# Entry into a state-space block: an order of steps for its first pair, another PSUM ring for its side line, other buffers for its time-step weights

## The chip, the cores and the metric

The kernel runs on one core of one Trainium2 chip. The metric is the device time of one execution in microseconds (us); less is better. Three executions of the kernel before took 2607.37, 2610.11 and 2611.04 us; their median is 2610.11 us. One more execution was taken with the profiler running; all views of the profile are of that one.

TensorE is called PE in the profile, VectorE DVE, ScalarE ACT, GpSimd POOL, and the engine that issues the DMAs SP. "PEld" is the weight load of PE. Each engine works through its own instructions strictly in the order in which they stand; what it needs from another engine it waits for.

## The reference, cut to what matters

The reference runs two layers over 4 sequences of 256 tokens with 512 features. Every step has a residual connection and takes the layer norm of its input:

```python
x = x + _L0_attn_ref(_layernorm(x), ...)   # block 1: gated retention, 32 heads
x = x + _L0_ffn_ref(_layernorm(x), ...)    # block 2: router, 64 experts' biases
x = x + _L1_attn_ref(_layernorm(x), ...)   # block 3: state space, 128 heads of 64
x = x + _L1_ffn_ref(_layernorm(x), ...)    # block 4: adapters of rank 16
```

Block 3, where the change lies, is in essence:

```python
proj = x @ in_proj_w.T                    # gate 8192 | x 8192, B 1024, C 1024 | dt 128
hBC = silu(causal_conv4(proj[x, B, C]) + conv_b)
hs, B, C = split(hBC)                     # 128 heads of 64; 8 groups of 128
dt = clip(softplus(proj[dt] + dt_bias), 0, 100);  A = -exp(A_log)
# in chunks of 128 tokens, two per sequence:
Y = (C B^T * exp(segsum(dt * A))) (hs * dt) + carried state + hs * D
g = Y * silu(gate);  g = g * rsqrt(mean of g^2 over each group + eps) * norm_w
out = g @ out_proj_w.T
```

The time step `dt` of every head and token is needed before anything can be decayed, so the 128 rows of `in_proj_w` that make it (the time-step weights) are used ahead of all else in this block.

## The kernel before

**Halves.** The 8 token tiles are worked in two halves of 4 tiles (512 tokens). `k.xs[half]` holds the normalized, turned input as a high and a low part; every projection (`proj`, L200) is 12 matmuls with 512 columns: four pieces of the contraction times three products (high by high, low by high, high by low).

**Weights.** All large weights go through `Weights`: a DMA into a `raw` buffer on SP, then `split` (L138 on ACT for the high part, L141 on POOL for the low part) into rings of three buffers (tag "w") or two ("wo"). A cast into a ring buffer waits until PE has used the weight that was there.

**Block 3 in pairs.** One *pair* is one group, one pair of channel chunks and one half. The first eight pairs are four pairs of half 0 and then the same four of half 1 (`FIRST3 = 1`). For each `i` the loop in `run` overlaps three pairs: `before`, `p` and `after`. Its order is written out by hand as letters. `B` projects B and C of a group, convolves them (L707 ACT, L709 DVE) and makes the products `cb` (L728 PE, L732 ACT). `I0 I1` project and convolve x, `G0 G1` project the gates (tile `ps_g`, silu on ACT), `X0 X1` load the cumulated decays and add them up (`exponents`, L286, L293, L295), `D0 D1` exponentiate them and multiply by `cb` (L1110 ACT, L748 DVE). `T0 T1` turn x (L770, L772, L781), `M0 M1` are the mixing matmuls `ps_y` (L795) with L805, L809, L813 and L814 behind them, `O0` to `O3` are the output projection `ps_o` (L849, L855). `W` takes the next weight, `P` and `E` pump the side line.

**The side line.** Work that belongs to other blocks is a list of generators, `k.side`, and is worked off in small steps in between. As soon as a half has left block 1, `route(half)` (block 2) and then `prepare3(half)` (L676: time-step weights, layer norm, `steps_of` for dt and its cumulated sum) are put on it. While block 3 works on its first pairs, half 1 is still in the side line: its router (`ps_xn` L107, `ps_lg` L596, a softmax and top 8 on DVE, `ps_t` L627, `ps_o` L642), its norm (`ps_xn` again) and its time steps (`ps_dt` L200, `ps_v` L220, `ps_cum` L249, `ps_in` L258, `ps_tail` L267). All of them must be through before the first pair of half 1. Every step of the side line takes its PSUM tile from the ring that `k.bank` names. There are four rings of two banks each: "x" (projections of x, B, C, and `cb`), "g" (gates), "y" (turned x and `ps_y`), "o" (output). In block 1 the side line uses "o"; in block 3, and in the preparation of block 4 that runs beside its last pairs (`prepare4`), it uses "x". `first(c)` of block 4 always takes ring "g".

**Which list holds.** At `i = -1` there is no pair to mix yet and only `after` has work:

```python
STEP3 = "W T0 T1 B I0 W M0 M1 X0 X1 I1 O0 G0 W W O1 W W P O2 W W G1 P W O3 D0 D1 W W".split()
SIDE3 = "T0 T1 I0 I1 M0 M1 P B X0 X1 P P O0 W O1 G0 G1 W W P O2 O3 W P W P D0 D1 E E".split()
for one in SIDE3 if k.side else STEP3:
```

**Scheduler.** The letters give the order of the program. A scheduler then places the instructions on the engines' queues by its own model of their durations, within what the tiles' buffers allow: a tile in a ring of two can't be written before the tile two places earlier in that ring has been read.

Of the kernel before, what the change touches and what calls it, by code (L numbers as in the profile page):

```python
# [11 lines left out]
F32 = mybir.dt.float32  # L12
F32R = mybir.dt.float32r
AF = mybir.ActivationFunctionType
ALU = mybir.AluOpType
# [3 lines left out]
P = 128  # L19
NB, SEQ, HID = 4, 256, 512  # L20
NT = NB * SEQ // P
KC = HID // P
HT = NT // 2
FREE = HT * P
EPS = 1e-5
GONE = -30000.0
YB = 3
LONE1, FIRST3, LONE3 = 3, 1, 2
PUMP = 1
AHEAD = 0  # L30
BANK1, BANK3 = "o", "x"
LATE = (0, 3)
STEP1 = "K S0 W T S1 S2 W G0 G1 K C K P U A0 K W P A1 T P P Q0 N0 W W N1 Q1 T T W K D F".split()
SIDE1 = "S0 W G0 T P K C W W P P W S1 K G1 S2 U P A0 N0 A1 P Q0 T W T F W N1 K Q1 T T D W W".split()
STEP3 = "W T0 T1 B I0 W M0 M1 X0 X1 I1 O0 G0 W W O1 W W P O2 W W G1 P W O3 D0 D1 W W".split()
SIDE3 = "T0 T1 I0 I1 M0 M1 P B X0 X1 P P O0 W O1 G0 G1 W W P O2 O3 W P W P D0 D1 E E".split()


# [72 lines left out]
def normalize(k, tc, half, tag, into=("xn",)):  # L111


    nc = tc.nc
    tiles = [HT * half + at for at in range(HT)]
    of = [moments(k, tc, t, tag) for t in tiles]
    ahead = len(into)
    xns = [centre(k, tc, tiles[at], of[at], tag, into[at]) for at in range(ahead)]
    yield
    for at, t in enumerate(tiles):  # L120
        xn = xns[at]
        ps = turned(k, tc, xn, f"xn_{tag}_{t}")
        hi, lo = (part[:, :, at * P:at * P + P] for part in k.xs[half])
        nc.scalar.copy(hi, ps)
        nc.vector.tensor_tensor(lo, ps, hi.bitcast(F32), ALU.subtract)
        if at + ahead < HT:
            xns.append(centre(k, tc, tiles[at + ahead], of[at + ahead], tag, into[at % ahead]))
        yield


def split(k, tc, w, name, tag, late=False):

    nc = tc.nc
    n = w.shape[1]
    bufs = 3 if tag == "w" else 2
    hi = k.wp.tile([P, 2, HID], F32R, tag=tag + "h", name=f"{name}_h", bufs=bufs)[:, 0:n, :]
    lo = k.wp.tile([P, 2, HID], F32R, tag=tag + "l", name=f"{name}_l", bufs=bufs)[:, 0:n, :]
    high = nc.scalar.copy(hi, w)  # L138
    if late:
        tc.keep_in_program_order(high)  # L140
    nc.gpsimd.tensor_tensor(lo, w, hi.bitcast(F32), ALU.subtract)  # L141
    return hi, lo
# [506 lines left out]
def state_space(k, tc, io):  # L649


    nc = tc.nc
    NH, NG, D = 128, 8, 64
# [22 lines left out]
    def prepare(half):  # L676

        if half == 0:
            yield True
            k.act(amp, amp, AF.Exp)  # L680
            nc.vector.tensor_scalar_mul(amp, amp, -1.0)
        raw = k.wk.tile([P, 1, FREE], F32, tag="xn", name=f"raw_wdt_{half}", bufs=1)
        nc.sync.dma_start(raw, io["L1_attn_in_dt"])
        yield
        wd = split(k, tc, raw, f"wdt_{half}", "w")
        yield from normalize(k, tc, half, "3")

        def room(size, name):
            if half == 0:
                return k.const.tile([P, size], F32, name=f"{name}3_0")  # L690
            return own.only.tile([P, size], F32, name=f"{name}3_1")

        dt[half] = room(HT * NH, "dt").rearrange("p (t h) -> p t h", t=HT)
        start[half] = room(3 * 2 * NH, "start").rearrange("p (k h b) -> p k h b", k=3, b=2)
        yield from steps_of(
            k, tc, half, [part[:, 0, :].rearrange("p (c m) -> p c m", c=KC) for part in wd], NH,
            bias, amp, 100.0, dt[half].rearrange("p (b z) h -> p b z h", b=2), start[half],
            cum[half], "3", "y" if half else "a",
        )
        ready.add(half)  # L700
# [14 lines left out]
    def group(p):  # L715

        g, half = p.g, p.half
        bc = [
            k.wk.tile([P, FREE], F32, tag="y", name=f"bc_{g}_{half}_{n}", bufs=4) for n in range(2)
        ]  # L720
        for n, first in enumerate((BS, CS)):
            conv(proj(k, tc, chunk(p.w.bc(), n), half, f"bc_{g}_{half}_{n}"), bc[n], first + g)
        s = own.only.tile([P, 3, 2, P], F32, tag="cb", name=f"cb_{g}_{half}", bufs=2)
        for b in range(2):
            ps = k.psum.tile([P, 3, P], F32, tag="x", name=f"ps_cb_{g}_{half}_{b}")
            for n, (zs, zl) in enumerate(((0, 0), (1, 1), (0, 1))):
                fs, fl = (2 * b + zs) * P, (2 * b + zl) * P
                nc.tensor.matmul(  # L728
                    ps[:, n, :], bc[0][:, fs:fs + P], bc[1][:, fl:fl + P],
                    start=True, stop=True,  # L730
                )
            nc.scalar.copy(s[:, :, b, :], ps)  # L732
        cbs[g, half] = s

    def sums(p, n):
        hs = slice(2 * (p.ch + n), 2 * (p.ch + n) + 2)
        p.e[n] = exponents(
            k, tc, cum[p.half][:, hs, :], start[p.half][:, :, hs], f"{p.name}_{n}", 2
        )
# [15 lines left out]
    def inputs(p, n):  # L755
        xs = k.wk.tile([P, FREE], F32, tag="a", name=f"xs_{p.name}_{n}", bufs=4)
        conv(proj(k, tc, chunk(p.w.x(), n), p.half, f"x_{p.name}_{n}"), xs, p.ch + n)
        p.xs.append(xs)

    def gate(p, n):  # L760
        sg = k.wk.tile([P, FREE], F32, tag="sg", name=f"sg_{p.name}_{n}", bufs=4)
        k.act(sg, proj(k, tc, chunk(p.w.g(), n), p.half, f"g_{p.name}_{n}", "g"), AF.Silu)
        p.sg.append(sg)
# [73 lines left out]
    def output(p, t):  # L837
        if p.cp == 0 and t == 0:
            acc[p.g, p.half] = k.wk.tile([P, HT, HID], F32, tag="big", name=f"acc_{p.name}")
        if p.cp == NC // 2 - 1 and t == 0:  # L840
            scale(p)
        ps = k.psum.tile([P, HID], F32, tag="o", name=f"ps_o3_{p.name}_{t}")
        at = slice(t * P, t * P + P)
        i = 0
        for n in range(2):
            yh, yl = p.y[n]
            wh, wl = p.w.o()
            for y, w in ((yh, wh), (yh, wl), (yl, wh)):
                nc.tensor.matmul(ps, y[:, at], w[:, n, :], start=(i == 0), stop=(i == 5))  # L849
                i += 1  # L850
        a = acc[p.g, p.half][:, t, :]
        if p.cp == 0:
            nc.scalar.copy(a, ps)
        else:
            nc.vector.tensor_tensor(a, a, ps, ALU.add)  # L855
        if p.cp == NC // 2 - 1:
            xt = k.x[HT * p.half + t]
            nc.vector.scalar_tensor_tensor(xt, a, p.r[:, t:t + 1], xt, ALU.mult, ALU.add)  # L858
# [8 lines left out]
    for together in order:  # L867
        pair = [(*divmod(n, NC // 2), half) for half in range(2) for n in together]
        for g, cp, half in pair:
            p = Ctx()  # L870
# [13 lines left out]
    def run(done):  # L884


        with tc.tile_pool(name="s3", bufs=1, reuse_waits="tile") as own.only:
            for i in range(-1, len(pairs) + 1):
                k.bank = BANK3
                before, p, after = (  # L890
                    pairs[j] if 0 <= j < len(pairs) else None for j in (i - 1, i, i + 1)
                )
                if i + 2 < len(pairs):
                    k.weights.due = pairs[i + 2].w.g.n
                else:
                    k.weights.due = len(k.weights.all) - 1
                if after is not None and after.half not in ready:
                    k.pump(1000, True)

                def shared():  # L900
                    if after.cp == 0:
                        group(after)

                def put(t):
                    output(before, t)
                    if t == HT - 1 and all(one.half != before.half for one in pairs[i:]):
                        done(before.half)

                step = dict(
                    B=shared, I=lambda n: inputs(after, n), G=lambda n: gate(after, n),  # L910
                    X=lambda n: sums(after, n), D=lambda n: decays(after, n), T=lambda n: turn(p, n), M=lambda n: mixer(p, n),
                    O=put, W=k.weights.step, P=k.pump, E=lambda: k.pump(1, True),
                )
                for one in SIDE3 if k.side else STEP3:
                    who = {"T": p, "M": p, "O": before, "P": k, "E": k, "W": k}.get(one[0], after)
                    if who is not None and (i >= 0 or not AHEAD or one[0] not in "IG"):
                        step[one[0]](*(int(n) for n in one[1:]))

    def ahead(i):
# [8 lines left out]
        else:  # L928
            sums(p, n)

    return ahead, prepare, run


# [309 lines left out]
```

## Time and profile before

| | |
|---|---|
| median of three executions | 2610.11 us (2607.37 to 2611.04) |
| the profiled execution | 2612.82 us, of which the span from first to last instruction is 2611.1 us |
| busy: PE, DVE, ACT, POOL | 2475.6, 2082.7, 1533.4, 1530.1 us |
| mean granted TensorE clock | 0.978 |
| first matmul of block 3 | 923.2 us after the start |
| first projection of block 3 from which both kernels' PE queues are alike again (second x of group 1, pair 0, half 1) | 1238.8 us |
| last matmul | 2607.2 us |

A row of "busy time in stretches" gives a stretch, its length, the busy time of PE, PE's weight loads, DVE, ACT and POOL with their instruction counts, the granted TensorE clock, the busy share of the DMA engines and their rate. Rows of a timeline give the start, the duration, the engine, the line, the operation with its output and inputs, the number of instructions, and in square brackets how long the engine stood idle before it and who released it. Durations of matmuls are pipelined: 12 projection matmuls that stand one behind another take 2.80 us together, although each row says 0.40 us.

### The profile page before, as it was taken

The numbers are of one execution on the slowest core, as the hardware profiler recorded it, in microseconds if no ns is written. First come the engines' busy times: TensorE is split into PE (matmuls) and PEld (weight loads), VectorE is DVE, ScalarE is ACT, GpSimd is POOL, SyncE is SP. The second block draws the span as 40 slices with busy tenths as digits, with TensorE's granted clock in tenths as the row PEclk, the third lists the DMA queues.
The fourth block names the chain that finished last, engine by engine and source line by source line (L and its number), as shares of the span: only waits on it lengthen the run. The fifth ranks groups of instructions, "written<-read, shape, count | busy, mean of one in ns | idle before, by whom it ended". The sixth has DMA issues, their size and how long they took to land.

```text
span 2611.1 us, 35577 instructions
## 1 busy us (share of the span) xinstructions
PE 2475.6 (95%) x13488; PEld 2001.8 (77%) x13488; DVE 2082.7 (80%) x2694; ACT 1533.4 (59%) x2109; POOL 1530.1 (59%) x996
## 2 busy tenths in 40 slices
PE   7899999999999888889999999999999999999889
PEld 5677787788777676668878788788787887887667
DVE  5678777778789767688897988888888878879963
ACT  2556556566665555465765665756757657657631
POOL 4445444546565445577674874765756766757840
PEclk9899999999999988999999999999999999999989
DMA  3212111212221222232322222323222222313221
GB/s 105 74 49 65 57 49 56 58 59 87 88 93 57 77 89 69 69 108 86 98 90 65 89 89 68 103 65 89 95 75 89 89 69 88 101 61 104 90 77 67
DMA packets 82891, 206.18 MB, mean 79 GB/s; under 512 B 8672, under 2 KB 10592, under 8 KB 82720
## 3 DMA queue, kind: packets, MB, share of 16 engines
q1 hardware_dynamic: 82720, 203.90, 25.3%
q8 instruction: 107, 1.75, 0.3%
q14 instruction: 64, 0.52, 0.1%
HBM read 200.86 MB, written 3.01 MB: 78 GB/s over the span
## 4 chain that ended last, share of the span: by engine, by line
PE 60%; DVE 24%; ACT 6%; POOL 5%; issue 4%; DMA 2%; SPq 0%; POOLq 0%; ACTq 0%; DVEq 0%
PE ps_g L200 12%; PE ps_o L849 8%; PE ps_x L200 6%; PE ps_o L458 6%; PE ps_q L200 6%; DVE conv L709 5%; DVE m L748 5%; PE ps_y L795 3%; PE ps_y L411 3%; PE ps_sc L399 2%; DVE x L858 2%; PE ps_bc L200 2%; DVE m L293 2%; PE ps_v L200 2%; PE ps_h L200 2%
## 5 line engine op out<-in xcount | busy, mean ns | idle before, releaser
L200 PE MATMUL ps_g<-xs_hi,wg_h 128*128 128x512 f32 x768 | 309.8, 403 | 17.5 <-ACT wg_h L138 7.3
L200 PE MATMUL ps_g<-xs_lo,wg_h 128*128 128x512 f32 x768 | 305.5, 398 | 0.0
L200 PE MATMUL ps_g<-xs_hi,wg_l 128*128 128x512 f32 x768 | 304.1, 397 | 1.2 <-POOL wg_l L141 1.2
L748 DVE TENSOR_TENSOR m<-m,cb 128x1536 f32<-128x1536 f32 x128 | 263.8, 2073 | 47.8 <-ACT m L1110 43.4
L709 DVE SCALAR_TENSOR_TENSOR conv<-ps_x,cw,conv 128x510 f32<-128x510 f32 (+2 forms) x384 | 271.1, 739 | 17.6 <-ACT conv L707 14.4
L1107 ACT ACT_TABLE_LOAD x193 | 247.6, 1283 | 4.0 <-PEq L1231 0.8
L141 POOL TENSOR_TENSOR wo_l<-raw_wo,wo_h 128x1024 fp32r<-128x1024 f32 x60 | 154.6, 2578 | 136.6 <-ACT wo_h L138 136.5
L293 POOL TENSOR_TENSOR m<-gb,start 128x512 f32<-128x512 f32 x128 | 152.9, 1197 | 137.6 <-PE ps_y L795 94.4
L1110 ACT ACTIVATE xs<-conv,cb 128x512 f32<-128x512 f32 x128 | 91.8, 724 | 239.6 <-DVE conv L709 236.6
L809 POOL TENSOR_TENSOR xs<-xs,sg 128x512 f32<-128x512 f32 x128 | 201.2, 1572 | 42.9 <-DVE xs L805 42.3
L849 PE MATMUL ps_o<-wo_h,yh 128*128 128x512 f32 x512 | 213.0, 416 | 9.8 <-DVE acc L855 6.9
L295 POOL TENSOR_SCALAR_AFFINE_SELECT m<-m 128x1024 f32<-128x1024 f32 x160 | 216.7, 1355 | 0.8 <-DVE m L293 0.7
L200 PE MATMUL ps_x<-xs_hi,wx_h 128*128 128x512 f32 x512 | 206.4, 403 | 7.8 <-DVE conv L709 7.8
L849 PE MATMUL ps_o<-wo_h,yl 128*128 128x512 f32 x512 | 201.1, 403 | 6.3 <-DVE yl L814 6.2
L200 PE MATMUL ps_x<-xs_lo,wx_h 128*128 128x512 f32 x512 | 204.9, 400 | 0.0
L200 PE MATMUL ps_x<-xs_hi,wx_l 128*128 128x512 f32 x512 | 203.6, 398 | 0.0
L849 PE MATMUL ps_o<-wo_l,yh 128*128 128x512 f32 x512 | 203.2, 397 | 0.0
L823 POOL TENSOR_TENSOR sqs<-sqs,sq 128x512 f32<-128x512 f32 x112 | 174.7, 1560 | 48.5 <-ACT sq L821 48.1
L141 POOL TENSOR_TENSOR wx_l<-raw_wx,wx_h 128x1024 fp32r<-128x1024 f32 x38 | 97.8, 2575 | 174.4 <-DVE conv L709 118.7
L795 PE MATMUL ps_y<-m,xd 128*64 128x128 f32 x2048 | 178.2, 280 | 14.5 <-DVE m L748 13.8
L141 POOL TENSOR_TENSOR wg_l<-raw_wg,wg_h 128x1024 fp32r<-128x1024 f32 x60 | 159.1, 2652 | 54.8 <-ACT wg_h L138 52.8
L200 PEld LDWEIGHTS ps_g<-xs_hi,wg_h 128*128 128x128 f32 x768 | 144.8, 189 | 60.2 <-issue 14.9
(281 smaller groups left out, 6975.0 us busy)
## 6 DMA issues: line engine op xcount, KB each, us to landing
gb<-cum SPq DMA_DIRECT2D x160, 512.0 KB
raw_wx<-in_L_attn_in_x_dram SPq DMA_DIRECT2D x38, 512.0 KB
raw_wg<-in_L_attn_in_gate_dram SPq DMA_DIRECT2D x38, 512.0 KB
raw_wo<-n_L_attn_out_proj_w_dram SPq DMA_DIRECT2D x38, 512.0 KB
raw_wq<-in_L_attn_Wq_dram SPq DMA_DIRECT2D x22, 512.0 KB
raw_wg<-in_L_attn_Wg_dram SPq DMA_DIRECT2D x22, 512.0 KB
raw_wo<-in_L_attn_Wo_dram SPq DMA_DIRECT2D x22, 512.0 KB
raw_wkv<-in_L_kv_dram SPq DMA_DIRECT2D x11, 512.0 KB
```

Source lines behind the costliest of these rows:

```text
L141: nc.gpsimd.tensor_tensor(lo, w, hi.bitcast(F32), ALU.subtract)
L200: tc.nc.tensor.matmul(ps, a[:, c, :], b[:, c, :], start=(c == 0 and n == 0), stop=(c == KC - 1 and n == 2))
L293: engine.tensor_tensor(m[:, blk], gb[:, min(blk, 1)], last(at, P), ALU.add)
L295: nc.gpsimd.affine_select(out=causal, in_=causal, compare_op=ALU.is_ge, fill=GONE, base=0, pattern=[[0, 8], [1, P]], channel_multiplier=-1,)
L458: nc.tensor.matmul(ps, y[:, 2 * h + b, :], w[:, h, :], start=(i == 0), stop=(i == 5))
L709: nc.vector.scalar_tensor_tensor(acc[:, :, j:], ps[:, :, :SEQ - j], cw[:, ch, TAPS - 1 - j:TAPS - j], acc[:, :, j:], ALU.mult, ALU.add,)
L748: made = nc.vector.tensor_tensor(mh, mh, cbs[p.g, p.half].rearrange("p z b l -> p z (b l)").unsqueeze(2) .to_broadcast([P, 3, 2, 2 * P]), ...
L795: one = nc.tensor.matmul(ps_y[h * D:h * D + D, 2 * b + z, :], p.xe[:, n, b, h, :] if blk == 2 else xd[:, 2 * b + zs, h, :], m[:, blk, 2 * ...
L809: nc.gpsimd.tensor_tensor(xs, xs, p.sg[n], ALU.mult)
L823: nc.gpsimd.tensor_tensor(total, total, sq, ALU.add)
L849: nc.tensor.matmul(ps, y[:, at], w[:, n, :], start=(i == 0), stop=(i == 5))
L1107: load = nc.scalar.preload_act_table_set(table)
```

## The change

1. At `i = -1` the loop follows a list of its own, `FILL3`: the decays' loads first, B and C ahead of x, and the side line's steps at other places.
2. `BANK3` is "g" instead of "x": the side line of block 3, and the preparation of block 4 that runs beside it, take their PSUM tiles from the gates' ring.
3. The time-step weights of `prepare3` no longer go through `split` and the ring "w". For half 0 the raw block and its two parts take free buffers of the tags "yh" and "yl"; for half 1 the raw block goes into the first 512 columns of `k.room` (the tables of sine and cosine of block 1) and the parts into the ring "y" of four. Tag "xn" no longer holds the raw block.

```diff
-BANK1, BANK3 = "o", "x"
+BANK1, BANK3 = "o", "g"
...
+FILL3 = "X0 X1 B I0 W I1 P P G0 G1 W P P D0 D1 E E".split()
...
-        raw = k.wk.tile([P, 1, FREE], F32, tag="xn", name=f"raw_wdt_{half}", bufs=1)
-        nc.sync.dma_start(raw, io["L1_attn_in_dt"])
+        if half == 0:
+            raw = k.wk.tile([P, FREE], F32, tag="yh", name="raw_wdt_0", bufs=YB)
+        else:
+
+            raw = k.room[:, 0:FREE]
+        nc.sync.dma_start(raw, io["L1_attn_in_dt"][:, 0])
         yield
-        wd = split(k, tc, raw, f"wdt_{half}", "w")
+        tags, bufs = (("yh", "yl"), YB) if half == 0 else (("y", "y"), 4)
+        wd = [
+            k.wk.tile([P, FREE], F32R, tag=tag, name=f"wdt_{half}_{part}", bufs=bufs)
+            for tag, part in zip(tags, "hl")
+        ]
+        nc.scalar.copy(wd[0], raw)
+        nc.gpsimd.tensor_tensor(wd[1], raw, wd[0].bitcast(F32), ALU.subtract)
         yield from normalize(k, tc, half, "3")
...
-            k, tc, half, [part[:, 0, :].rearrange("p (c m) -> p c m", c=KC) for part in wd], NH,
+            k, tc, half, [part.rearrange("p (c m) -> p c m", c=KC) for part in wd], NH,
...
-                for one in SIDE3 if k.side else STEP3:
+                for one in FILL3 if i < 0 else SIDE3 if k.side else STEP3:
```

The number of instructions is the same on every engine. On PE the two kernels' queues are alike up to the last gate of block 1, and again from the projection at 1238.8 us to the first turned tile of block 4.

## Prediction

> **What bounds the kernel now.** I read the totals by engine first, then the slices, then PE's busy time by stretches, then the timeline of PE wherever a stretch was short of it.
>
> ```profile
> PE 2475.6 (95%) x13488; PEld 2001.8 (77%) x13488; DVE 2082.7 (80%) x2694; ACT 1533.4 (59%) x2109; POOL 1530.1 (59%) x996
> PE   7899999999999888889999999999999999999889
> PEclk9899999999999988999999999999999999999989
> ```
>
> PE is the bound nearly everywhere; slices 14 to 18 (849 to 1175 us; block 3 begins at 923) are one of the few weak spots, and in 15 and 16 the granted clock falls too. The stretches show where:
>
> ```profile
> 923.21:960.50 37.29, 37.29 (x175) 30.59 (x173) 26.45 (x38) 21.74 (x30) 17.72 (x10) 1.00 0.21 72
> 960.50:985.10 24.60, 15.70 (x86) 13.38 (x85) 11.13 (x18) 8.53 (x13) 6.55 (x10) 0.58 0.25 85
> 1000.80:1017.00 16.20, 14.20 (x36) 7.71 (x35) 10.51 (x17) 10.14 (x15) 6.37 (x9) 0.68 0.31 97
> 1033.00:1064.00 31.00, 20.14 (x77) 14.80 (x75) 23.31 (x26) 13.36 (x19) 13.75 (x8) 0.82 0.27 85
> 1064.00:1235.86 171.86, 160.36 (x965) 127.88 (x964) 140.72 (x159) 102.09 (x140) 126.26 (x73) 0.98 0.30 93
> 1240.00:1400.00 160.00, 158.03 (x963) 127.76 (x963) 141.34 (x169) 106.40 (x145) 106.06 (x66) 1.00 0.28 84
> ```
>
> No engine is full in rows two to four (columns: stretch, length, then PE, weight loads, DVE, ACT, POOL): these are chains that PE waits for. Its timeline names them:
>
> ```profile
> 881.18 0.47 PE L200 MATMUL ps_g<-xs_hi,wg_h 128*128 128x512 f32 x1 [2.61 <-DVE r_q L353]
> 966.39 1.11 PE L107 MATMUL ps_xn<-ident,xn 128*128 128x128 f32 x4 [4.06 <-ACT cb L732]
> 972.18 1.12 PE L107 MATMUL ps_xn<-ident,xn 128*128 128x128 f32 x4 [2.03 <-DVE xn L99]
> 1004.80 7.13 PE L642 MATMUL ps_o<-room,wT 64*128 64x512 f32 x8 [1.99 <-ACT wT L629]
> 1040.30 1.22 PE L849 MATMUL ps_o<-wo_h,yl 128*128 128x512 f32 x2 [3.86 <-DVE yl L814]
> 1043.73 0.76 PE L200 MATMUL ps_dt<-xs_hi,wdt_h 128*128 128x512 f32 x1 [2.22 <-DVE xs_lo L125]
> 1063.36 0.79 PE L200 MATMUL ps_g<-xs_hi,wg_h 128*128 128x512 f32 x1 [3.94 <-ACT wg_h L138]
> ```
>
> The third row is a side step that waits for a bank of ring "x" still held by `cb`; the fourth is router work at half clock (8 matmuls in 7.13 us); the next two are the layer norm and output projection before the time steps. The dt chain itself follows: `ps_v`'s copy starts at 1053.86 and the last `e` before `ps_cum` ends at 1063.73, 9.9 us of DVE and ACT.
>
> **How much PE loses at the entry.** Full-clock prices come from dense rows: 12 projection matmuls 2.80 us (0.2335 each), `ps_y` 0.121, a transpose 0.11, four `cb` 0.87. From 923.21 to 1235.86 stand 832 matmuls of 512 columns (194.3), 216 `ps_y` (26.1), 112 transposes (12.3), 24 `cb` (5.2), 16 router logits (3.4), 24 small ones (4.7) and 6.1 of `o2`, `ps_in` and `ps_tail`: 252 us of work in 312.65, so 60.5 are lost. Where: nothing in the first stretch; 24.6 less 8.2 of work = 16.4; 16.2 less 7.2 = 9.0; 31.0 less 15.6 = 15.4; 3 between them; 16.5 behind 1064. In the regular pairs (last row, 158.03 of 160) the loss is about 1%. An idle stretch also costs behind itself: after 2.61 us idle (row at 881.18) the 12 matmuls took 4.44 instead of 2.80, so 1.7 more; 0.84 us idle at 1053.16 cost nothing.
>
> [...]
>
> **The change, part by part.** All counts of instructions stay, so only waits and order change.
>
> *Time-step weights at the start.* Being out of ring "w", half 0's cast moves from about 798 us to the start: its 256 KB load now stands ahead of the first `wg` load, which in before issues only at 18.40 us for want of a raw buffer; the ACT cast (0.6) falls into 5.57 us in which ACT idles before 22.06; POOL's part (1.35) pushes `wg_l` from 23.2 to 24.55, and PE wants it near 26.9. Cost 0, at most 1 if that slack is gone. At 798 us a cast of 0.61 on ACT and 1.35 on POOL vanish and later weights take ring buffers one place sooner; no PE wait there is traced to them: 0, within 1 either way. For half 1 the parts stand in ring "y" of four; their loads no longer wait for "w" or "xn". PE's queue is the same from there to 923, so 0.
>
> *The entry, by the new order.* Before's queue at 923 starts with x, x, B, C, the first `y1` tile, gates, output projections, and only then the router. After's is B, C, `y1`, `m1`, the 24 output matmuls of block 1's last unit, `cb`, the router transposes, gates, x, x, gates, and the router's steps spread among projections. I put before's durations on after's queues, each instruction starting when its engine, its inputs and its ring buffer are free, by hand. PE's waits:
>
> W1, about 937: the last unit of block 1 has its norm in the open. `sq` and `sh` 0.60 each, Ln and Exp with a table load (0.65, 0.63, 1.283), `rms` 0.9, `yh` 0.62, `yl` 0.69, with B's convolution on DVE between: 4.9 idle in two pieces (in before, gates and x covered this) plus 1.7 cold = 6.6.
> W2, 943 to 975, the router: xn 0.55, xT 0.59 and the softmax no longer wait for `cb`; PE waits 1.1 + 0.75 + 0.85, with projections between = 2.8. Before lost 25.4 on the router's two stretches.
> W3, `o3` waiting on `yh` and a neighbour: 1.7.
> W4, about 1010: a gate tile waits for the bank that `o2_4` holds in ring "g"; the DVE add that empties it stands behind POOL's `by`, behind a weight part of 2.40: 4 to 5 idle, 4.9 taken, plus 1.8 cold = 6.7.
> W5, the norm's `xn_3` transposes and `m` of the first pair (L748, 1.74 to 3.26 us a piece): 5.5.
> W6, gates on `xs_lo`, and `o3` on `yh` again: 3.4.
> W7, the dt chain: between `ps_v` and `ps_cum` stand only 9 output matmuls (2.1), where before had 24 of x and 4 of gates (6.5). DVE's queue between them has its 12 steps plus 4 of convolution, 12.2 us. 12.2 − 2.1 = 10.1, plus 2.2 cold = 12.3.
>
> Sum 39. At the same amount of PE work (113 us behind 923) before has lost 44: a lead of 5.
>
> W8, the remainder to the aligned projection (before 1238.8): before loses another 16.5, among it 3.34 idle at 1147.62. After gets there with DVE some 10 us further in its own list (25 instructions more done by the time `ps_cum` starts), so fewer such waits; between 2 (as in the regular pairs) and 16.5 (the row from 1064 on) I take the middle, 9, since both rows are alike near. The entry: 5 + 7.5 = 12.5 saved. Bounds: W1 to W7 at half and at one and a half of their size give ±19 as extremes, but they share durations that were measured, so ±10 is taken, with W8 ±7.
>
> *The end.* `prepare4` takes ring "g", which `first(c)` of block 4 uses too. So the first weight transposes `t4_0` stand behind the third `ps_h` of unit 0 instead of the seventh: their softmax chain starts 4.7 us sooner (2504.4 against 2509.06), but `ps_h` queued behind them wait about 4.4, plus 2 cold. Against that, block 4's gates are loaded some 6.6 us earlier; in before the stretch that follows is weak:
>
> ```profile
> 2500.00:2545.00 45.00, 39.79 (x174) 31.53 (x175) 24.25 (x65) 15.20 (x25) 11.34 (x13) 0.92 0.22 74
> ```
>
> Waits of 1.02, 2.19 and 2.00 at 2528.6 to 2540 and 11 logits in 5.06 instead of 2.6 are its loss, about 7. The last four norm tiles come later, however, and the loads of two gates go into buffers that these free. Net +2.5 taken, from −3 (all of the stall covered) to +6 (none).
>
> Sum: −12.5 + 2.5 = −10.0. The profiled execution took 2612.8 (span 2611.1 and 1.7 around it), 2.7 above the median: 2612.8 − 10.0 − 2.7 = 2600.1.
>
> **Rivals.**
> *Lockstep in ring "g" (slower, 2623).* Ring "g" now serves gates and side line in turn, in the order of the queue; a side tile of a DVE chain holds the gates' bank. Price per blocked step: 4.06, the idle of the `cb` row, plus 1.7 cold, 5.8. Of 22 side tiles (4 `xn` twice, `lg` 2, `t` 2, `o2` 4 and six of the time steps) I have charged two or three (W4, W6). Two further blocked steps (11.6) take the gain away, and from three on (17.4) this decides; I price it with four, one of each kind: −10 + 23.2 = +13.2, so 2623. For: the gates stand closer to side tiles than x did, and the g ring's reader for gates is ACT, which has table loads of 1.283 in between. Against: ACT is 59% busy, and a silu of 0.596 empties a gate bank at once, where `conv` on DVE held x's.
> *Given back (same, 2609.6).* The new fill uses projections early that before had for the later chains. If W1 and W7 each cost half as much again (9.5 in all), −10 + 9.5 = −0.5 is left. For: DVE has 80% of the span, and its queue at W7 carries four steps of convolution among the chain.
> *Both holes close (faster, 2587).* The chain W7 overlaps with the output matmuls, W1 with B's projections, and W8 falls to 2: −7 for W8, −6.3 for a third of W1 and W7. For: block 1's last unit may be normalized earlier than by my walk, since its DVE steps no longer stand behind x's convolution.
> *The change does nothing (2610).* Only if the order were the scheduler's anyway; PE's queue differs in some 1250 places, so this has little.
>
> **How the numbers follow.** Chances: forecast 0.44, both holes close 0.19, given back 0.18, lockstep 0.18, nothing 0.01. The forecast's own range is 2590 to 2605: ±10 by the waits, cut where the given-back case begins. The range from 2585 to 2615 adds the given-back case, both-holes down to 2 us under its price, and the lockstep case only where fewer steps block; it leaves out some 0.2. A measurement of this kernel can tell about 0.2%, 5.2 us, from no change: faster (below 2604.9) has the forecast and both-holes, 0.63; same has given back but for 0.01, and nothing, 0.18; slower has lockstep and that 0.01, 0.19.
>
> **What would show it.** Right (lines of before): an idle of some 5 us before `ps_o` L458 at 937 to 942, ended by ACT `yh` or DVE `yl`; the router's transposes and logits at a clock near 1.00; one idle of 4 to 5 us of `ps_g` ended by DVE x L644; about 10 us before `ps_cum` L249, ended by DVE `e` L245; 4 us before `t4_0` at L994; the aligned projection near 1226 instead of 1238.8. Wrong: many waits of `ps_g` on readers of side tiles (lockstep); the projection at 1238 or later; a wait for `wg_l` at 27 us; or the loss at the end above 6.

## The result, and the profile after

The changed kernel takes 2614.94 us (median of nine, 2609.48 to 2620.79) against 2609.63 for the kernel before; the ratio is 1.0025, with a 95% interval of 1.0013 to 1.0037. It is slower by 3 to 10 us, where 10 less had been forecast. Its profiled execution has a span of 2615.0 us.

The page's totals and slices (line 1 of the fence: busy time; 2 and 3: PE's busy tenths and the granted clock in 40 slices):

```profile
PE 2474.1 (95%) x13488; PEld 2001.6 (77%) x13488; DVE 2076.6 (79%) x2694; ACT 1531.7 (59%) x2109; POOL 1523.8 (58%) x996
PE   7899999999999888899999999999999999999889
PEclk9899999999999989899999999999999999999999
```

The weak spot is where it was. Busy time by stretches (stretch, length, then PE, weight loads, DVE, ACT, POOL, then clock, DMA share, GB/s):

```profile
923.10:956.60 33.50, 26.68 (x118) 21.54 (x117) 22.10 (x34) 17.01 (x25) 13.57 (x11) 0.85 0.15 48
956.60:1004.00 47.40, 45.40 (x253) 36.60 (x253) 29.98 (x43) 27.59 (x38) 21.86 (x16) 0.93 0.24 75
1004.00:1040.00 36.00, 26.56 (x134) 18.60 (x128) 30.51 (x48) 14.18 (x21) 23.57 (x25) 0.91 0.28 93
1071.00:1094.00 23.00, 14.46 (x57) 10.60 (x56) 15.94 (x24) 9.74 (x14) 4.75 (x2) 0.78 0.30 85
1094.00:1238.50 144.50, 138.57 (x832) 111.99 (x832) 112.92 (x130) 85.16 (x118) 105.35 (x62) 0.98 0.31 97
2500.00:2545.00 45.00, 37.13 (x157) 28.39 (x158) 23.71 (x63) 13.78 (x23) 10.78 (x12) 0.92 0.20 63
```

The router's stretch, which before had PE at 15.70 of 24.60 us with a clock of 0.58, now runs almost full (second row). In exchange the first stretch, full before, has a hole of 7 us, and there are deeper ones at 1004 and 1071. PE's timeline names them; lines are 1 higher than before up to the new code, 11 higher behind it:

```profile
937.12 0.50 PE L436 MATMUL ps_m<-sh,mean 128*128 128x512 f32 x1 [1.03 <-ACT sh L427]
940.04 0.80 PE L437 MATMUL ps_m<-sl,mean 128*128 128x512 f32 x1 [2.42 <-DVE sl L428]
944.21 0.80 PE L459 MATMUL ps_o<-wo_h,yh 128*128 128x512 f32 x1 [3.37 <-ACT yh L446]
1031.74 0.80 PE L201 MATMUL ps_g<-xs_hi,wg_h 128*128 128x512 f32 x1 [6.07 <-DVE x L644]
1085.41 0.58 PE L250 MATMUL ps_cum<-upper,e 128*128 128x128 f32 x1 [8.54 <-DVE e L246]
2518.18 0.61 PE L1005 MATMUL ps_t<-ident,lg 128*64 128x128 f32 x2 [4.80 <-DVE lg L1002]
```

These are the waits that were forecast, in their order: the bare norm, the gate behind an `o2` bank, the dt chain, `t4_0`. The aligned projection stands at 1241.4, not 1226 (1238.7 in the kernel before).

To compare kernels whose queues differ I use **lost time by work done**: the time since the first matmul of block 3, less the full-clock prices (those of the prediction) of all matmuls issued since. "Entry" and "end" below are differences to the kernel before, in one profile each, of the time from that first matmul to the aligned stretch (1246), and from a matmul at 2461 to the last one. Kernels whose PE queues are the same there agree within some 2 us, but for the entries of e2 and e9, whose other engines have other work. In e1, e2, e7, e9, e12 and e15 the order differs until 1303; counted to there, their entries are some 0.5 us lower. "Measured" is the ratio to the kernel before on the same chip, in us of 2610, with its interval; a difference between two such rows is uncertain by some 4 us.

| kernel | lost at 20 us of work | at 60 | at 80 | at 120 | at 260 | entry | end | measured |
|---|---|---|---|---|---|---|---|---|
| before | 1.9 | 21.5 | 26.9 | 42.1 | 57.2 | 0 | 0 | 0 |
| changed | 12.4 | 18.5 | 29.7 | 50.5 | 60.7 | +3.5 | +3.5 | +6.5 (3.4 to 9.7) |
| e1 gates first | 3.5 | 13.5 | 22.6 | 43.4 | 53.1 | -1.8 | +5.1 | +1.0 (-1.6 to 3.9) |
| e2 `by` on ACT | 12.4 | 18.4 | 23.1 | 46.9 | 56.6 | +3.3 | +2.7 | +4.4 (1.8 to 7.0) |
| e3 end on "x" | 12.5 | 18.6 | 28.1 | 50.2 | 60.5 | +3.3 | -0.2 | +2.9 (0.5 to 5.5) |
| e4 list + weights | 3.5 | 15.2 | 24.3 | 50.3 | 60.7 | +3.5 | -0.2 | +2.6 (-0.3 to 5.2) |
| e5 ring g | 5.5 | 23.5 | 31.3 | 42.7 | 54.1 | -3.1 | +6.7 | +5.5 (2.9 to 7.8) |
| e6 weights | 1.9 | 26.0 | 33.0 | 48.5 | 74.9 | +17.8 | -1.2 | +12.5 (9.4 to 15.7) |
| e7 = e1 + e3 | 3.5 | 14.6 | 24.0 | 44.1 | 53.7 | +0.4 | -1.0 | -1.0 (-3.4 to 1.3) |
| e8 = e7 + two P | 3.5 | 15.0 | 27.0 | 38.8 | 49.7 | -7.5 | +5.4 | -0.8 (-3.1 to 1.6) |
| e9 list + ring g | 12.3 | 18.3 | 28.1 | 53.5 | 63.2 | +10.0 | +4.5 | +12.8 (9.7 to 16.2) |
| e10 list | 3.5 | 14.2 | 24.0 | 49.3 | 61.2 | +4.1 | -1.4 | +5.7 (3.1 to 8.6) |
| e11 ring g + weights | 4.7 | 22.8 | 36.4 | 46.9 | 59.8 | +2.6 | +7.9 | +8.4 (5.2 to 11.5) |
| e12 e8, old weights | 3.5 | 15.9 | 24.4 | 38.7 | 49.9 | -3.4 | +0.2 | -4.7 (-7.0 to -2.1) |
| e13 parts of half 1 | 1.9 | 26.1 | 33.0 | 47.7 | 74.6 | +17.5 | -0.8 | +15.7 (12.0 to 19.1) |
| e14 raw of half 1 | 1.9 | 24.3 | 32.8 | 48.8 | 65.1 | +7.9 | +0.3 | +3.1 (0.8 to 5.7) |
| e15 e12 + half 0, raw | 3.5 | 15.5 | 24.9 | 39.4 | 51.5 | -3.4 | -1.2 | -4.2 (-6.3 to -1.8) |

Between 1246 and 2461, where the queues are all but the same, the profiles still differ by 0 to 9 us, so a single profile's total says nothing of a change this size; the stages say more.

### The profile page after: what moved, and what is told of

Read it like the earlier page. It is cut to its first block, busy times and chain, and to the rows that moved or that the text cites. A ratio compares the mean times of both kernels' runs of the same rounds, so it can differ in the third digit from the quotient of the medians.

```text
span 2615.0 us, 35558 instructions
## 1 busy us (share of the span) xinstructions
PE 2474.1 (95%) x13488; PEld 2001.6 (77%) x13488; DVE 2076.6 (79%) x2694; ACT 1531.7 (59%) x2109; POOL 1523.8 (58%) x996
## 4 chain that ended last, share of the span: by engine, by line
PE 60%; DVE 24%; POOL 5%; ACT 5%; issue 4%; DMA 3%; SPq 0%; POOLq 0%; ACTq 0%; DVEq 0%
PE ps_g L201 13%; PE ps_o L860 8%; PE ps_x L201 7%; PE ps_o L459 6%; PE ps_q L201 5%; DVE m L759 5%; DVE conv L720 4%; PE ps_y L806 3%; PE ps_y L412 3%; PE ps_sc L400 2%; DVE x L869 2%; PE ps_bc L201 2%; DVE m L294 2%; PE ps_v L201 2%; DVE yl L825 2%
## 5 line engine op out<-in xcount | busy, mean ns | idle before, releaser
L820 POOL TENSOR_TENSOR xs<-xs,sg 128x512 f32<-128x512 f32 x128 | 200.2, 1564 | 40.0 <-DVE xs L816 39.4
```

The costliest lines, as they stand in the source:

```text
L820: nc.gpsimd.tensor_tensor(xs, xs, p.sg[n], ALU.mult)
```

## The experiments

**The bare norm (e1).**

```diff
-FILL3 = "X0 X1 B I0 W I1 P P G0 G1 W P P D0 D1 E E".split()
+FILL3 = "X0 X1 B I0 W I1 G0 G1 P P W P P D0 D1 E E".split()
```

> The changed kernel, with G0 G1 moved ahead of the two P in FILL3. Theory (ring g in the order of the list): the side line's xn_2_4 takes its bank of ring g before the first gates do, so the gates may not be placed ahead of it, and the norm of block 1's last unit stands bare (11.8 us lost between 933 and 956 in the changed kernel). With the gates first, 24 gate matmuls (5.6 us) stand between the statistics and the output matmuls: the three waits of 1.03, 2.42 and 3.37 us shrink to 2 us or less together, and the lost time by 20 us of work from 12.4 to 5 or 6. The total falls by 3 to 6 us against the changed kernel, less than the 6 or 7 of the hole because those gates no longer lie beside the router. Rival (the list's early X0 X1 and B alone make the hole, through DVE's m<-gb in 2.73 us): the waits stay above 5 us together and the total within 2 us of the changed kernel.

The queue now has 24 gate matmuls between the first statistics `ps_m` and the output matmuls of block 1's last unit. PE's waits there:

```profile
939.74 0.50 PE L437 MATMUL ps_m<-sl,mean 128*128 128x512 f32 x1 [0.84 <-DVE sl L428]
946.70 0.50 PE L459 MATMUL ps_o<-wo_h,yh 128*128 128x512 f32 x1 [0.49 <-ACT yh L446]
```

They fall from 6.8 to 1.3 us, 8.9 us less are lost by 20 us of work, 7.6 of it is still there at 260 and 5.8 at 1303, behind one more wait; the total falls from +6.5 to +1.0. The theory holds: with the side line in ring "g", its first tile `xn_2_4` stood ahead of the gates in the ring's order, so nothing could fill the hole. DVE's `m<-gb,start`, the rival's cause, stands in the same place in e1 and takes 2.78 us there, no less than in the changed kernel, so it does not make the hole by itself. (The two intervals of the totals just overlap; it is the stage that shows the effect.)

**The slow `x<-x,by` (e2).** These four scale x by the router's result; they stand before the adds that empty the `o2` banks.

```diff
-            nc.vector.tensor_scalar(k.x[t], k.x[t], by[:, 0, at:at + 1], by[:, 1, at:at + 1], ALU.mult, ALU.subtract)
+            nc.scalar.activation(k.x[t], k.x[t], AF.Identity, scale=by[:, 0, at:at + 1], bias=by[:, 1, at:at + 1])
```

(for half 1 alone, with the sign of `by[:, 1]` turned on POOL)

> The changed kernel, with the four x<-x,by of half 1 on ACT instead of DVE. Theory (DVE is blocked beside POOL): in the changed kernel these four take 7.11 us on DVE at 1023.4, where POOL runs two weight parts of 2.36 and 2.52 us and a sum of squares; in the kernel before the same four took 2.68. On ACT they take about 2.4 us, the o2 banks come free 4 us sooner, and the wait of the gates (6.07 us at 1031.7) falls to 1 to 2.5 us; the total falls by 3 to 6 us. Rival (lockstep in ring g: the gates wait for the order of the ring, not for the length of these four): the wait stays above 4 us, or comes back at the next side tile, and the total is within 2 us.

DVE's row in the kernel before, then DVE and POOL in the changed kernel:

```profile
992.58 2.68 DVE L638 TENSOR_SCALAR x<-x,by 128x512 f32<-128x512 f32 x4
```
```profile
1023.39 7.11 DVE L639 TENSOR_SCALAR x<-x,by 128x512 f32<-128x512 f32 x4 [0.20 <-POOL by L637]
```
```profile
1025.37 2.36 POOL L142 TENSOR_TENSOR wbc_l<-raw_wbc,wbc_h 128x1024 fp32r<-128x1024 f32 x1 [0.59 <-ACT wbc_h L139]
1027.69 2.52 POOL L142 TENSOR_TENSOR wo_l<-raw_wo,wo_h 128x1024 fp32r<-128x1024 f32 x1
```

On ACT the four take 2.93 us and the gate's wait falls from 6.07 to 1.54:

```profile
1026.26 0.50 PE L201 MATMUL ps_g<-xs_hi,wg_h 128*128 128x512 f32 x1 [1.54 <-DVE x L651]
1036.32 1.11 PE L108 MATMUL ps_xn<-ident,xn 128*128 128x128 f32 x4 [2.29 <-DVE xn L100]
1040.84 0.47 PE L108 MATMUL ps_xn<-ident,xn 128*128 128x128 f32 x1 [3.40 <-DVE xn L100]
```

6.6 us less are lost by 80 us of work. Some 2.2 of it are chance: the changed kernel's profile has a wait for a convolution that is all but gone in e2, and in e3 too, where every engine's queue is that of the changed kernel up to there (changed, then e3):

```profile
1012.70 0.50 PE L201 MATMUL ps_x<-xs_hi,wx_h 128*128 128x512 f32 x1 [2.46 <-DVE conv L720]
```
```profile
1013.65 0.50 PE L201 MATMUL ps_x<-xs_hi,wx_h 128*128 128x512 f32 x1 [0.30 <-DVE conv L720]
```

In the one DVE's `m<-gb,start` takes 2.83 us beside a weight part of POOL, in the other 0.68. But the last two `o2` matmuls still stand behind two gate tiles in ring "g", and the norm that needs them waits 2.29 and 3.40 where it waited 1.30 and 0.69; 3.6 are left at 120, and another wait for a convolution at 1243 takes back most of that: entry +3.3, total 2 us less than the changed kernel, inside both intervals. Most of this one wait is explained; as a saving it does not last, so the rival is half right.

**The end (e3).**

```diff
-                k.bank = BANK3
+                k.bank = BANK3 if i < 8 else "x"
```

> The changed kernel, with ring x for everything that the side line does from the ninth pair on, so prepare4 has the ring that it had in the kernel before. The entry is untouched. Theory (the end costs 3.5 us of the difference by itself): the 4.80 us wait before t4_0 at 2518 vanishes, the last 130 us run like the kernel before's, and the total falls by 3 to 4 us against the changed kernel, to about 2 to 3 us above the kernel before. Rival (the end evens out and the difference is all from the entry): total within 1 us of the changed kernel.

The wait before `t4_0` is gone, the end is that of the kernel before (-0.2), the total 3.6 less, as expected. The six profiles with ring "g" at the end read +2.7 to +7.9 there, those with ring "x" -1.4 to +0.3, but for one (e8, +5.4). So ring "g" costs the end some 3 us or more; how much more differs with the company.

**One, two and three parts of the change (e4, e5, e6, e9, e10, e11).** The list is `FILL3`, ring g is `BANK3 = "g"`, the weights are the new buffers; each kernel takes the hunks of the change named in the table.

> The changed kernel, with ring x for the side line throughout; FILL3 and the places of the time-step weights stay. Theory (ring g costs, the list itself does not): the gates fill the norm of block 1's last unit again, so less than 3 us are lost by 20 us of work instead of 12.4; the router's tiles wait for x and cb as in the kernel before (some 10 us over its four tiles); the end is as before, -3.5. In sum 4 to 8 us less than the changed kernel, so 0 to 3 us less than the kernel before. Rival (the list costs: with two P fewer at the entry the side line is late for the first pair of half 1): the lost time by 120 us of work is above 50 us as in the changed kernel, and the total at or above it.

> The kernel before, with ring g for the side line as the only edit. Theory (ring g has two prices and one gain): in the order of this queue the gates of the first pair stand behind the router's first tile, so the norm of block 1's last unit has only B's projections as cover: 4 to 6 us lost by 20 us of work against 1.9 before; the router's tiles no longer wait for cb (4.06 us) and win some of it back; the end costs 3.5 as in the changed kernel. In sum 2 to 6 us above the kernel before. Rival (ring g alone is free and the list is what costs): within 1.5 us of the kernel before.

> The kernel before, with the time-step weights in their new places as the only edit. Theory (the move is neutral by itself): the first 100 us run within 1 us of the kernel before, the end is the same, and of the entry only what lies behind the router changes; total within 2 us of the kernel before. Rival (the move is what brings the side line forward, since the parts no longer wait for a buffer of ring w): the 15 us lost between 1033 and 1064 shrink by 4 us or more and the total is 3 us or more below the kernel before.

> The changed kernel with the time-step weights back in split, ring w and tag xn (list and ring g stay). Theory (half 1's weight parts in ring y cost here too, since ring y also holds the products' B and C, which may then be written only after ps_dt): the entry loses 3 to 6 us less than in the changed kernel between the time steps and the aligned projection, and the total is 3 to 6 us below the changed kernel, near the kernel before. Rival (the move hurts only with the old list): total within 2 us of the changed kernel, the idle before ps_cum again 8 us.

> The kernel before with FILL3 as the only edit. Against the run with list and weights in ring x it tells the weights' price in a third company: between ps_v and ps_cum stand 22 gate matmuls (5.1 us) where there it is 11 matmuls. Theory (cover decides): the idle before ps_cum is 3 to 5 us instead of 8.9, the entry loses about 5 us less than with the weights moved, total 1 to 4 us below the kernel before. Rival (the list costs, by its two P fewer): the entry loses 3 us or more above the kernel before's and the total is above it.

> The changed kernel with the old list at the entry (ring g and the weights stay). Theory (the weights' move costs about 12 us under the old list, whichever the ring): total 10 us or more above the kernel before, as with the weights alone. Rival (what made the weights alone slow is x ring's waits, which ring g takes away): 3 to 7 us above the kernel before, as with ring g alone.

Measured against the kernel before: list +5.7, ring g +5.5, weights +12.5; list and ring g +12.8, list and weights +2.6, ring g and weights +8.4; all three +6.5. The single prices add up to 23.7, so they do not add. Run by run:

- e4: the norm is covered (3.5, nearly as expected), but by 120 us of work 50.3 are lost: the rival's figure. PE waits 5.60 us for a gate's bank (`sg`, ACT) and 8.92 before `ps_cum`. It is 3.9 us below the changed kernel, nearly all of it the end; the theory had it at or below the kernel before, the rival at or above the changed kernel, so neither has the total.
- e5: total in the expected range, but at the wrong place: the entry is 3.1 better than before, and the end 6.7 worse. By the profile ring g has its price at the end. That profile, though, is of the fastest of twelve executions, 2606.70 us, where the others took 2617.43 to 2623.00, so this division is not shown for them.
- e6: both theories missed. See e13.
- e9: both missed. Taking the weights back costs 6.3 us more than the changed kernel; the wait before `ps_cum` grows from 8.54 to 11.84:

```profile
1089.32 0.58 PE L250 MATMUL ps_cum<-upper,e 128*128 128x128 f32 x1 [11.84 <-DVE e L246]
```

- e10: with 22 gate matmuls as cover the wait before `ps_cum` is 6.01, less than 8.92 but more than expected, and the total is above before's: the rival.
- e11: 8.4, with an interval that reaches into both theories; it doesn't tell them apart.

**Repairs together (e7, e8, e12).** e7 has e1's list and e3's line. e8 adds two P; e12 is e8 with the weights where they were before:

```diff
+FILL3 = "X0 X1 B I0 W I1 G0 G1 P P W P P P D0 D1 P E E".split()
```

> The changed kernel with the gates first in FILL3 and ring x for the side line from the ninth pair on: both repairs together. Theory (two separate prices, which add): -5.6 at the entry and -3.6 at the end against the changed kernel, so 2 to 4 us less than the kernel before. Rival (one is given back when the other is gone): no more than 1 us below the kernel before.

> As both repairs together, and with two more P in FILL3 (W P P P D0 D1 P E E), which brings the router's end and the time steps some 80 PE instructions forward. Theory (the wait for the dt chain before ps_cum is a lack of cover, not a matter of when the side line runs): between ps_v and ps_cum stand only 5 matmuls of B and C (1.2 us), so the idle before ps_cum stays at 8 us or more, and the total is within 2 us of the kernel with both repairs. Rival (the side line is simply too late, since FILL3 has two P fewer than the list before): the idle before ps_cum falls below 5 us and the total by 4 us or more.

> The kernel before with ring g for the side line at the entry alone (ring x from the ninth pair on) and the list with the gates first and two more P; the weights stay where they were. Theory (cover and ring order decide, the weights' move is a loss): the norm is covered (3.5 us lost by 20 us of work), the idle before ps_cum is 5 to 7 us with 13 matmuls of B and C as cover, the end is the kernel before's; total 3 to 7 us below the kernel before. Rival (what is won early is given back at the next wait for DVE): total within 2 us of the kernel before.

e7 is at -1.0, and the sum of both repairs would be -2.6; its interval holds theory and rival. e8's wait before `ps_cum` is 8.30 and its total that of e7, as the theory has it: pumping sooner does not shorten a chain without cover. (Its entry is 7.9 better than e7's in the profiles and its end 6.4 worse, with another order on PE in both; with one profile each I leave that open.) e12 is the only kind of kernel that beats both: -4.7 us, ratio 0.9982 (0.9973 to 0.9992). By 40 us of work it has lost 4.8 where before had lost 15.0. Its total and its cover of the norm are as expected, but not the wait before `ps_cum`, 10.09 us where 5 to 7 were expected. The dt chain still stands bare, so more would be to be had there:

```profile
1056.23 0.58 PE L250 MATMUL ps_cum<-upper,e 128*128 128x128 f32 x1 [10.09 <-DVE e L246]
```

**Which part of the weights' move (e13, e14, e15).**

```diff
 e13
-        wd = split(k, tc, raw, f"wdt_{half}", "w")
+        if half == 0:
+            wd = split(k, tc, raw, f"wdt_{half}", "w")
+        else:
+            wd = [k.wk.tile([P, 1, FREE], F32R, tag="y", name=f"wdt_{half}_{part}", bufs=4) for part in "hl"]
+            nc.scalar.copy(wd[0], raw)
+            nc.gpsimd.tensor_tensor(wd[1], raw, wd[0].bitcast(F32), ALU.subtract)
 e14 (half 1)
-        raw = k.wk.tile([P, 1, FREE], F32, tag="xn", name=f"raw_wdt_{half}", bufs=1)
+        raw = k.room[:, 0:FREE].rearrange("p (o f) -> p o f", o=1)
```

> The kernel before, with half 1's two weight parts in ring y as the only edit (its raw block stays in tag xn, half 0 stays as it was). Theory (the parts are what moves the queues: they no longer wait for ring w, so the scheduler takes the layer norm and the time steps in another order against the output projections, and the products' B and C have fewer buffers in ring y): about the 12 us of the whole move, 8 to 15 us above the kernel before, most of it lost between 1180 and 1245 in waits of ps_o and ps_y for DVE. Rival (the raw block's new place or half 0's move do it): within 3 us of the kernel before.

> The kernel before, with half 1's raw weights in k.room instead of tag xn as the only edit. Theory (the raw block's place is nearly free; it lets the load be issued sooner and frees xn for the norm): within 3 us of the kernel before. Rival (it is what costs): 8 us or more above.

> The kernel with all repairs (list with gates first and two more P, ring g at the entry alone), and in addition half 0's weights at the start and half 1's raw block in k.room; half 1's parts stay in ring w. PE's order is the same as without them. Theory (both are neutral, as they move no PE instruction): 3 to 6 us below the kernel before, within 2 us of the kernel with all repairs. Rival (they start the time steps sooner): 2 us or more below it.

The parts are it: +15.7 alone, with e6's losses at the same places; the raw block costs 3.1 (0.8 to 5.7; its entry of +7.9 is from the slowest of its twelve executions), half 0's move and the raw block add nothing to e12 (-4.2 against -4.7). In e13 the aligned projection stands at 1255.9. Shortly ahead of it, where the PE queues still differ, PE waits 4.74 us at 1243; the kernel before has no such wait there. DVE, POOL and PE in e13:

```profile
1236.47 2.80 DVE L293 TENSOR_TENSOR m<-gb,start 128x512 f32<-128x512 f32 x1
1240.57 2.50 DVE L822 SCALAR_TENSOR_TENSOR yl<-xs,nw,yh 128x512 fp32r<-128x512 f32 x1
```
```profile
1236.33 2.39 POOL L141 TENSOR_TENSOR wo_l<-raw_wo,wo_h 128x1024 fp32r<-128x1024 f32 x1
1240.19 2.34 POOL L141 TENSOR_TENSOR wg_l<-raw_wg,wg_h 128x1024 fp32r<-128x1024 f32 x1
```
```profile
1243.13 1.22 PE L857 MATMUL ps_o<-wo_h,yl 128*128 128x512 f32 x2 [4.74 <-DVE yl L822]
```

Two weight parts fall beside two DVE steps; both end 0.5 us after POOL's (1239.27 after 1238.72, 1243.07 after 1242.53). In the kernel before the same two steps took 1.48 us (at 1227.12) and 1.59 (at 1229.78), between two weight parts that ran from 1221.97 to 1224.34 and from 1230.78 on. So the weight parts explain at most some 2.2 us of this wait. Where the rest of it and e13's other losses come from is not settled.

## Why the prediction was wrong

The entry had been put at 39 us lost by the end of the dt chain and 44 for the kernel before, a lead of 5. Measured at 120 us of work: 50.5 and 42.1, a lag of 8.4. That step of the sum failed, and with it the sign; the waits themselves came where they were forecast. Its terms:

- **W1**, 6.6 forecast, 11.8 measured (0.6 lost at 10 us of work, 12.4 at 20): one of the two mis-sized terms. The idle is 6.82 instead of 4.9, because DVE's `m<-gb,start` stood ahead of `sl` and took 2.73 us instead of 0.7, beside a weight part on POOL:

```profile
935.81 2.73 DVE L294 TENSOR_TENSOR m<-gb,start 128x512 f32<-128x512 f32 x1
```
```profile
935.64 2.35 POOL L142 TENSOR_TENSOR wx_l<-raw_wx,wx_h 128x1024 fp32r<-128x1024 f32 x1 [3.22 <-PE ps_y L412]
```

  The rest, 5.0, was put at 1.7 of cold clock. More than half of it is: the 24 output matmuls behind the last wait took 8.31 us (944.21 to 952.52) instead of 5.6, and the two `ps_m` between the waits 0.8 too much. Some of what is left the kernel before loses too, without a wait (1.9 by 20 us of work). The granted clock (third number from the right) through these waits:

```profile
937.10:940.00 2.90, 0.50 (x1) 0.19 (x1) 2.90 (x4) 1.18 (x2) 2.83 (x3) 0.97 0.29 86
940.00:944.20 4.20, 0.80 (x1) 0.29 (x1) 3.23 (x6) 3.27 (x5) 0.94 (x1) 0.50 0.17 67
944.20:949.50 5.30, 5.29 (x13) 4.15 (x14) 2.68 (x5) 0.67 (x2) 0.00 (x0) 0.50 0.00 0
```

  The fault of method was to take the waits one by one with a fixed cold charge: between these three PE worked 0.5 and 0.8 us, and the clock, down from 940 on, came back only near 950.
- **W4**, 6.7 forecast, about 11.8 measured (18.5 at 60 us of work; 30.3 at 82): the other one. The forecast wait itself is 6.07 instead of 4.9. In the same stretch PE also waits 2.46 us for a convolution, 0.55 and 0.32, of which the sum has nothing; the 2.46 is the chance wait of 1012.70 shown at e2. And the 6.07 is near the forecast partly by luck: `x<-x,by` was walked with the 2.68 it took in the kernel before, where no weight part lay beside it, 4.4 us too little, and without that the wait is 1.54 (e2). The walk had the rest of this chain too long. The duration of a DVE step belonged here to its place (2.68 and 7.11 us for the same four), not to its line.
- W2 and W3 4.5 forecast, 6.1 measured; W5 and W6 8.9 and 10.7; **W7** 12.3 and 9.5. Of the right size.
- **W8**: 9 forecast, 10.2 measured, against 15 in the kernel before: near. The 9 was the middle between two bounds far apart, and no run tests the reason given (DVE further ahead).
- **The end**: a wait of 4.4 forecast, 4.80 measured, net 2.5 against 3.5; e3 gives 3.6 by the times. Right, within the spread named at e3.
- **The weights**: taken as free at the start and at 798, and the entry was walked with them. Half 0's cost nothing beside e12's list and ring (e15). Half 1's parts are not: +15.7 alone, but worth 6.3 beside list and ring g (e9).

Of the rivals, lockstep in ring "g" named the right resource but not the right form: it expected tiles blocked while running, and the dearest effect found was in the order of the queue, where the gates were no longer allowed ahead of the router's tile (e1, 5.5 us). "Given back" named W1 and W7; W1 came 5.2 dearer, but W7 2.8 cheaper, and W4 was not among them. The time fell between the two.

On the clock: the granted clock was 0.50 from 940 on, after waits of 1.03 and 2.42 us with 0.50 us of work between them (rows above); the third wait, 3.37 us, came only then. So the cold charge of W1 was due although its idle came in pieces, and it was too small. How long a wait has to be for that, no run shows.

## What to carry to other kernels

When side work changes its ring of buffers, read first which tiles now stand behind it in that ring's order: what used to fill a hole may no longer be placed there. Price a DVE step by what POOL runs beside it at its new place, for a row from the old place holds only what lay beside it there (here 2.68 us for `x<-x,by` at the old place, 7.11 at the new one). Parts of a change to a hand-tuned queue don't add, so test them in each other's company (here 5.7 + 5.5 + 12.5 make 6.5), and take the best combination from the chip.

## What the runs showed of the hardware

DVE steps with two inputs in SBUF that began while POOL was subtracting a weight part ended 0.5 us after it: 0.7 us became 2.73 (935.81), 2.80 and 2.50 (e13). In the profiles of the kernel before and of the changed kernel, 42 steps of this kind (`m<-gb,start` and `yl`) begin behind the start of a weight part with over 0.3 us of it left, and each ends 0.54 to 0.56 us after that part. `x<-x,by`, with one such input, was drawn out too: four that take 0.53 each at their shortest took 7.11 together, two beside weight parts and one beside a sum of squares, each of these three ending 0.3 us after POOL. The convolution steps, which read PSUM and one SBUF input, took 0.73 to 0.75 throughout, all 480 in each of the two profiles. In rows where DVE's step began first it was POOL's that took longer: in the kernel before `m<-gb,start` took 0.68 (1147.49) and the weight part that began 0.16 us behind it 2.77, and `yl` 0.74 (1491.10) and the part 0.12 us behind it 2.89, where most parts take 2.4.

In the kernel before a `yl` that began 0.06 us behind a weight part took 2.89 (1286.20), and one that began 0.11 us ahead of a part 0.75 (1674.31). But the starts do not always tell: in e2 `m<-gb,start` began 0.05 us behind the weight part and still took 0.68, in the changed kernel 0.10 us behind it and took 2.83 (1008.49). A tenth of a microsecond in the starts thus stands beside over 2 us of DVE's time, and in e3, whose queues are those of the changed kernel up to there, the same step took 0.68. What in the chip is behind this, no run shows.
